# Loads of expert_w by rows, and two weight steps moved from the q/k/v part into the attention, in a pre-norm attention and MoE kernel

## The chip, the cores and the metric

The kernel runs on one core of a Trainium2 chip. The metric is the device time of one execution in microseconds (us). Before the change three runs gave a median of 2413.64 us (2413.22 to 2415.35).

The core has five engines with a queue of instructions each: TensorE (PE in the profile; PEld is its loading of weights), VectorE (DVE), ScalarE (ACT), GpSimd (POOL) and SyncE (SP). DMAs are issued here from SP and from POOL. The profile's q1 is the queue of the former, q0 that of the latter; both are worked on by the same 16 DMA engines.

## The reference

x has 2 x 2048 tokens of 1024 values in float32. The layer is an attention with one head of width 256 and a feed-forward part with a shared path and a routed path, which has one expert matrix and a gate:

```python
qkv = einsum('bsc,cf->bsf', layernorm(x), Wqkv) + bqkv          # 1024 x 768
attn = softmax(einsum('bqd,bkd->bqk', q, k) / sqrt(256))
x = x + einsum('bqd,dc->bqc', einsum('bqk,bkd->bqd', attn, v), Wo) + bo
h = layernorm(x)
shared = relu(h @ up_w) ** 2 @ down_w                             # 1024 x 2048 x 1024
routed = ((h @ fc1_w) @ expert_w * sum_top2(h @ gate_w)) @ fc2_w  # 1024 x 512 x 512 x 1024
x = x + layernorm2(shared + routed)                               # with ln_gamma, ln_beta
```

## The kernel before

Each float32 factor is split into two float32r parts, a high one (a cast on ACT) and a low one (a subtraction on DVE or POOL: `split`, L140). A product is then three matmuls (`Pass3`, L117). The 4096 tokens are 8 blocks of 512 rows. The work has four stages.

First, `begin` (L456) loads expert_w and both halves of fc2_w, and multiplies them once: expert_w @ fc2_w, the "fold" (`fold`, L487; tile pf). For that it needs expert_w with its rows along the free axis, so TensorE transposes it in 16 pieces of 128 x 128 (L478), four into one PSUM bank, and a bank is split into `eh` and `el`. expert_w lies in SBUF as `ew`, 128 partitions by 4 row groups of 512. Its four loads (L461) take 128 columns of all four row groups each. The queue of SP goes on with four loads of fc2_w's first half (L463), four rows of x, fc2_w's second half, and Wqkv. POOL loads the q/k bias and a broadcast of the v bias (bv). The second pass of the fold is interleaved with the transposes of the first block of x.

Second, `a_block` runs eight times in the order 4, 5, 6, 7, 0, 1, 2, 3 (`order`, L455). `qkv_block` (L406) computes four tiles of v (pv), then q and k (pq), and between these parts `after` normalises the next block: each of its four tiles is transposed by DVE in pieces of 32 x 32 (L213), written to DRAM by POOL (`xt_d`, L218), and fetched back by POOL in another order (`xt`, L224). The fourth tile's fetch is issued last, and its split comes after the next block's first tile of v. q is written to `q_d` by POOL (L448). In the last q/k/v block `after` also loads q_d of the first two blocks by SP (L663), and then come two loads of Wo (L701).

Third, the attention: for n from 1 to 8 the loop interleaves the scores of block n (`scores`, tile ps, two PSUM banks, a running maximum on DVE, L560) with the products of block n-1 with v (`values`, tile po), and ends with `finish` and `project` of block n-1 (tile pw, four PSUM banks). In `project` (L627) SP loads the residual x into `xres`, POOL adds bo to it by an accumulating DMA (L633), DVE adds the product (L644), and SP writes the sum to DRAM. POOL issues all four of these additions of a block ahead of what follows in its queue. A small load of gate_w (`g_f`, L704) precedes block 0's, and ACT and DVE split it (L749) in the middle of the first attention block.

Fourth, the feed-forward part multiplies quarters of the weights and of the activations in seven products where eight would be usual. It needs sums of quarters of up_w with fc1_w (s = 0) and of down_w with the fold (s = 1). These sums are made in DRAM by POOL's DMAs alone, in 14 steps (`sum_step`, L385):

```python
    SUMS = [(s, q) for s in range(2) for q in (1, 3, 2, 4)]
    COPIES = SUMS + [(s, q) for s in range(2) for q in ((0, 0), (1, 0), (1, 1))]
    ADDS = dict(zip((4, 5, 6, 8, 9, 10, 11, 13), SUMS))
```

A step copies one quarter (2 MB of up_w or down_w and 0.5 MB of fc1_w or of the fold, L389), and steps 4, 5, 6, 8, 9, 10, 11 and 13 then add another quarter, or a sum made before, to an earlier copy (L397, two DMAs again). Steps 0, 1 and 2 are taken after the blocks i = 4, 5 and 6 of the q/k/v part (L697). The others are taken in the attention, at k = 2 and k = 8 of each n from 2 on (L742), and are placed on POOL's queue directly behind the last bo addition of the block projected before (`last[0]`). So on POOL's queue they stand like this, with the bo additions of block b written as bo b:

```
q/k/v i=4: 0    i=5: 1    i=6: 2
g_f, bo 0 | 3 4+ | bo 1 | 5+ 6+ | bo 2 | 7 8+ | bo 3 | 9+ 10+ | bo 4 | 11+ 12 | bo 5 | 13+ | bo 6, bo 7
```

A plus marks a step with an addition. The numbers stand for copies; the additions go to `SUMS` in the order of `ADDS`.

Of the kernel before, what the change touches and what calls it, by code (L numbers as in the profile page):

```python
# [17 lines left out]
P = 128  # L18
# [7 lines left out]
def kernel(  # L26
# [21 lines left out]
    nc = tc.nc  # L48
# [3 lines left out]
    LAT = fc1_w.shape[1]  # L52
# [5 lines left out]
    NLC = LAT // P  # L58
    NKC = S // P
    NB = W // P  # L60
    NBLK = NT // W
# [105 lines left out]
    def cols(w, i, n):  # L167

        return w.rearrange("(c p) i -> p c i", p=P)[:, :, ts(i, n)]
# [213 lines left out]
    last = [None]  # L383
# [22 lines left out]
    def qkv_block(n, wqkv, xT, parts, after):  # L406

        keep = n < BPB  # L410
        units = {a: (unit if n == BPB - 1 else ex_unit)(f"{a}{n}") for a in "kv"}
        if keep:
            kv[n] = [units["k"], units["v"]]
        got = {}

        def v_tile(t):
            pm = bank(psa, "pv")
            if t % 2 == 0:
                got["v"] = half("v")
            acc = Pass3(pm[:, :D], NCC)  # L420
            for c in range(NCC):
                acc.add(x_chunk(xT, c, ts(t, P)), piece(wqkv[2], c, D, slice(0, D)))
            vt = got["v"][:, ts(t % 2, D)]
            nc.vector.tensor_tensor(vt, pm[:, :D], bv_sb, ALU.add)
            flush()
            split_late(vt, *(hl(units["v"])[:, s, ts(t, D)] for s in range(2)))

        def qk_chunk(a, dc):
            i = "qk".index(a)
            pm = bank(psa, "pq")  # L430
            acc = Pass3(pm, NCC)
            for c in range(NCC):
                acc.add(piece(wqkv[i], c, D, ts(dc, P)), x_chunk(xT, c))
            bias = bqk_sb[:, i * NDC + dc : i * NDC + dc + 1]
            flush()
            if a == "q":
                if dc == 0:
                    got["q"] = row("q")
                nc.scalar.activation(got["q"][:, ts(dc, W)], pm, AF.Identity, bias=bias)
            else:  # L440
                h, l = (hl(units[a])[:, s, ts(dc, W)] for s in range(2))
                nc.scalar.activation(h, pm, AF.Identity, bias=bias)
                nc.vector.scalar_tensor_tensor(l, pm, bias, f32(h), ALU.add, ALU.subtract)

        for j, (a, i) in enumerate(parts):
            v_tile(i) if a == "v" else qk_chunk(a, i)
            if (a, i) == ("q", NDC - 1):
                nc.gpsimd.dma_start(out=q_d[n], in_=got["q"])  # L448
            after(j)
        flush()  # L450
        if not keep:
            for a, d in (("k", k_d), ("v", v_d)):
                nc.gpsimd.dma_start(out=d[n], in_=f32(units[a]))

    order = list(range(BPB, NBLK)) + list(range(BPB))  # L455
    def begin(wqkv, xT):  # L456

        ew, f2_0 = (unit(a, FP) for a in ("ew", "f2_0"))
        ev = ew.rearrange("p (c n) -> p c n", n=LAT)
        for i in range(NLC):  # L460
            nc.sync.dma_start(out=ev[:, :, ts(i, P)], in_=cols(expert_w, i, P))  # L461
        for i in range(NLC):
            nc.sync.dma_start(out=f2_0[:, ts(i, W)], in_=fc2_w[ts(i, P), 0:W])  # L463
        f2 = [f2_0]
        first = load_block(xf, order[0])
        f2.append(load("f2_1", cols(fc2_w, 1, W))[1])

        ws = {i: load(f"w{i}", cols(Wqkv, i, D)) for i in (2, 0)}
        rows = load_block(xf, order[1])
        ws[1] = load("w1", cols(Wqkv, 1, D))  # L470
        nc.gpsimd.dma_start(out=bqk_sb, in_=bqkv[0 : 2 * D].rearrange("(f p) -> p f", p=P))
        nc.gpsimd.dma_start(out=bv_sb, in_=bqkv[2 * D : 3 * D].partition_broadcast(P))

        eh, el = unit("eh"), unit("el")
        for mc in range(NLC):
            pt = bank(psc, "pt")
            for lc in range(NLC):
                nc.tensor.transpose(pt[:, ts(lc, P)], ew[:, ds(lc * LAT + mc * P, P)], ident)  # L478
            split(pt, eh[:, ts(mc, LAT)], el[:, ts(mc, LAT)])

        def split_f2(h, eng):
            f2h, f2l = unit(f"f2h{h}"), unit(f"f2l{h}")
            for mc in range(NLC):
                split(f2[h][:, ts(mc, W)], f2h[:, ts(mc, W)], f2l[:, ts(mc, W)], eng)
            return f2h, f2l

        def fold(f2hl, first=None):  # L487
            accs = [Pass3(bank(psa, "pf"), NLC) for _ in range(NLC)]
            for mc in range(NLC):
                if first:  # L490
                    first(mc)
                for lc in range(NLC):
                    accs[lc].add(
                        piece((eh, el), mc, LAT, ts(lc, P)), piece(f2hl, mc, W, slice(0, W))
                    )
            return accs

        def folded(h, accs):
            r = unit(f"fold{h}", FP)
            for lc in range(NLC):  # L500
                nc.scalar.copy(r[:, ts(lc, W)], accs[lc].ps)
            return r

        accs = fold(split_f2(0, nc.vector))
        stats = [row_stats(first[0])]
        for t in range(NB):
            if t + 1 < NB:
                stats.append(row_stats(first[t + 1]))
            normalise(first[t], stats[t])
            if t == 0:  # L510
                f2hl = split_f2(1, nc.gpsimd)
            elif t == 2:
                wqkv[2] = split_unit(*ws[2], nc.gpsimd)
        r = [folded(0, accs)]
        r.append(folded(1, fold(f2hl, lambda t: transpose_tile(first[t], t, xT))))
        wqkv[0] = split_unit(*ws[0])
        wqkv[1] = split_unit(*ws[1], nc.gpsimd)
        return NormBlock(rows), r
# [167 lines left out]
    with tc.manual_schedule():  # L686
        norm, fold = begin(wqkv, xT)
        x3 = lambda: None
        steps = list(range(len(COPIES)))
        for i in range(NBLK - 1):  # L690
            norm, xT, x3 = a_block(i, norm, xT, x3)
            if i == 0:
                for h in range(C // W):
                    nc.gpsimd.dma_start(
                        out=cols(fc2e, h, W), in_=fold[h].rearrange("p (c n) -> p c n", n=W)
                    )
            if i >= NBLK // 2:  # L697
                sum_step(steps.pop(0))
    a_block(NBLK - 1, None, xT, x3)

# [6 lines left out]
    for n in range(1, NBLK + 1):  # L707
# [4 lines left out]
        for k in range(NKC + lag):  # L712
            if n + 1 < NBLK:
                if k == 0:
                    q_row = load_row(q_d[n + 1])
                elif k == NKC // 2:
                    start(n + 1, q_row)
            if n < NBLK and k < NKC:
                scores(n, k)
            if k >= lag:  # L720
                values(n - 1, k - lag)
                if n == BPB and (k - LAG) % 4 == 3:
                    j = BPB + (k - LAG) // 4
                    kv[j].append(load_kv(f"v{j}", v_d[j], kv_home(j)))
            if n == 1 and k == 1:
                softmax(0, 0)
            if n == 1 and k % 2 and 1 < k < NKC:
                softmax(0, k // 2)
            elif n > 1 and k % 2 == 0 and k + 2 < NKC:
                softmax(n - 1, k // 2 + 1)  # L730

            if k == NKC // 2 and n in range(2, 2 + NB):
                xts.append(load_row(x1[0][ts(n - 2, P), :]))
            elif k == 5 and n in range(3, 3 + NB):
                xts[n - 3] = norm_row(xts[n - 3], nc.sync)
            elif n == NBLK:
                if k < NB:
                    xts[k] = fetch_tile(xts[k], nc.sync)
                elif k % 2 == 0 and k >= 6 and k < 6 + 2 * NB:
                    for h, p in enumerate(X):  # L740
                        split_x(xts, h, k // 2 - 3, X[p])
            if k in (2, 8) and n > 1 and steps:  # L742
                with tc.issue_after(last[0].ins):
                    sum_step(steps.pop(0))
            if n == 1 and k == NKC // 2:
                wo = unit("wo_h"), unit("wo_l")
                for dc in range(NDC):
                    split(wo_f[dc], *(v[:, ts(dc, C)] for v in wo))
                split(g_f, gate[:, :, 0:NE], gate[:, :, NE : 2 * NE])  # L749
            if k == NKC - 1:  # L750
                if n == BPB - 1:
                    for j in range(BPB, 2 * BPB):
                        kv[j] = [load_kv(f"k{j}", k_d[j], kv_home(j))]
                if n < NBLK:
                    row_max(n)
# [532 lines left out]
```

## Time and profile before

| | us |
|---|---|
| median of three runs | 2413.64 |
| the profiled execution, its time | 2414.37 |
| its span, first to last instruction | 2412.4 |
| TensorE busy in the span | 2348.1 |

The stages in the span, with TensorE's and VectorE's busy time and the share of the 16 DMA engines:

| stage | from to | PE busy | DVE busy | DMA share |
|---|---|---|---|---|
| loads, fold | 0 to 40 | 31.25 | 20.83 | 0.76 |
| q/k/v | 40 to 320 | 271.83 | 155.13 | 0.73 |
| attention | 320 to 800 | 467.37 | 382.69 | 0.87 |
| feed-forward | 800 to 2412 | 1577.63 | 904.89 | 0.75 |

A matmul's end is modelled in the profile and matmuls overlap, so a busy TensorE is not one at its peak; its idle time is what shows a wait. The granted clock of TensorE (PEclk, 1.00 at full speed) falls for a while after some waits. A line of the timeline has the start and the duration in us, the engine, the line of the kernel, the operation, the tile written and those read, and in brackets how long the engine stood idle before and what ended that. For a DMA the duration is that of its issue; when its data has landed is told by the view of the DMAs.

### The profile page before, as it was taken

The numbers are of one execution on the slowest core, as the hardware profiler recorded it, in microseconds if no ns is written. First come the engines' busy times: TensorE is split into PE (matmuls) and PEld (weight loads), VectorE is DVE, ScalarE is ACT, GpSimd is POOL, SyncE is SP. The second block draws the span as 40 slices with busy tenths as digits, with TensorE's granted clock in tenths as the row PEclk, the third lists the DMA queues.
The fourth block names the chain that finished last, engine by engine and source line by source line (L and its number), as shares of the span: only waits on it lengthen the run. The fifth ranks groups of instructions, "written<-read, shape, count | busy, mean of one in ns | idle before, by whom it ended". The sixth has DMA issues, their size and how long they took to land.

```text
span 2412.4 us, 29279 instructions
## 1 busy us (share of the span) xinstructions
PE 2348.1 (97%) x10704; PEld 1922.9 (80%) x10704; DVE 1463.5 (61%) x2168; ACT 1131.3 (47%) x1846; POOL 299.5 (12%) x450
## 2 busy tenths in 40 slices
PE   8999899999998999999999999999999999999998
PEld 7888778888787778777777877777888887788886
DVE  5566549888777466687736458653446663445545
ACT  5555445555544553666552274544135354314224
POOL 3222110012110010011210011110000010000001
PEclk9999999999999999999999999999999999999999
DMA  5867883999996666677997778897557798655695
GB/s 186 320 245 266 286 201 110 287 317 320 285 244 183 214 230 184 230 244 243 337 307 237 239 265 316 316 333 259 194 184 266 257 325 292 212 194 185 203 310 189
DMA packets 225807, 603.99 MB, mean 250 GB/s; under 512 B 18768, under 2 KB 80720, under 8 KB 223616
## 3 DMA queue, kind: packets, MB, share of 16 engines
q1 hardware_dynamic: 152160, 334.02, 40.5%
q0 software_dynamic: 73504, 268.11, 36.3%
q8 instruction: 85, 1.39, 0.2%
q14 instruction: 58, 0.48, 0.1%
HBM read 448.96 MB, written 210.76 MB: 273 GB/s over the span
## 4 chain that ended last, share of the span: by engine, by line
PE 69%; issue 12%; DVE 6%; DMA 5%; ACT 5%; POOL 2%; POOLq 0%; SPq 0%; ACTq 0%; DVEq 0%
PE pu L130 28%; PE pd L130 21%; PE po L130 6%; PE ps L130 6%; PE pw L130 3%; DMA w<-wt 2%; DVE xblk L213 1%; DMA xres<-in_L_attn_bo_dram 1%; PE pg L870 1%; ACT xrow L283 1%; PE pf L130 1%; PE pq L130 1%; ACT junk L271 1%; DMA w_p<-w 1%; DVE w L821 1%
## 5 line engine op out<-in xcount | busy, mean ns | idle before, releaser
L130 PE MATMUL pd<-w,sp 128*128 128x512 f32 x3336 | 769.6, 392 | 18.8 <-DVE sp L1044 8.7
L130 PEld LDWEIGHTS pd<-w,sp 128*128 128x128 f32 x3336 | 625.8, 188 | 161.5 <-DVE sp L1044 18.0
L130 PE MATMUL pu<-xh,w 128*128 128x512 f32 x2240 | 692.9, 390 | 1.5 <-DVE w L821 0.8
L130 PEld LDWEIGHTS pu<-xh,w 128*128 128x128 f32 x2240 | 419.2, 188 | 92.4 <-DVE w L821 2.3
L130 PE MATMUL pu<-xl,w 128*128 128x512 f32 x1120 | 436.5, 390 | 2.9 <-DVE xl L150 2.8
L130 PEld LDWEIGHTS pu<-xl,w 128*128 128x128 f32 x1120 | 210.2, 188 | 48.3 <-DVE xl L150 4.6
L1044 DVE TENSOR_TENSOR sp<-h,sp 128x512 fp32r<-128x512 f32 x238 | 162.4, 687 | 128.2 <-ACT sp L1039 127.9
L1039 ACT CAST sp<-h 128x512 fp32r<-128x512 f32 x238 | 145.6, 618 | 182.7 <-PE pd L130 132.8
L130 PE MATMUL ps<-q,k 128*128 128x512 f32 x768 | 196.9, 394 | 3.7 <-DVE max L560 3.6
L130 PE MATMUL po<-p,v 128*128 128x512 f32 x768 | 197.2, 396 | 1.2 <-ACT p L142 1.1
L813 ACT CAST w<-w 128x512 fp32r<-128x512 f32 x210 | 128.1, 617 | 149.1 <-DMA w<-wt 140.3
L821 DVE TENSOR_TENSOR w<-w 128x512 fp32r<-128x512 f32 x210 | 142.8, 685 | 88.7 <-ACT w L813 87.0
L130 PEld LDWEIGHTS ps<-q,k 128*128 128x128 f32 x768 | 143.0, 189 | 38.5 <-DVE max L560 9.0
L130 PEld LDWEIGHTS po<-p,v 128*128 128x128 f32 x768 | 144.8, 190 | 31.9 <-ACT p L142 1.5
L824 POOL DMA_DIRECT2D w_p<-w x140 | 75.7, 541 | 586.6 <-DVE w L821 525.9
L992 ACT ACTIVATE h<-h 128x1024 f32<-128x1024 f32 x48 | 50.6, 1055 | 208.0 <-DVE h L1091 159.7
L555 ACT COPY s<-ps 128x512 f32<-128x512 f32 x128 | 75.0, 586 | 152.3 <-PE ps L130 148.9
L150 DVE TENSOR_TENSOR xl<-xt,xh 128x512 fp32r<-128x512 f32 x104 | 71.6, 688 | 120.8 <-ACT xh L149 120.7
L213 DVE STREAM_TRANSPOSE xblk<-xrow 128x1024 f32<-128x1024 f32 x60 | 120.4, 2007 | 39.1 <-ACT xrow L283 36.4
L560 DVE TENSOR_TENSOR max<-ps,max 128x512 f32<-128x512 f32 x120 | 82.4, 687 | 45.2 <-ACT s L555 45.1
L130 PE MATMUL pq<-xha,w_h 128*128 128x512 f32 x256 | 99.7, 389 | 0.0
L130 PE MATMUL pq<-xha,w_l 128*128 128x512 f32 x256 | 99.7, 389 | 0.0
(181 smaller groups left out, 3040.7 us busy)
## 6 DMA issues: line engine op xcount, KB each, us to landing
w<-w_p SPq DMA_DIRECT2D x350, 512.0 KB, 4.3
w_p<-w POOLq DMA_DIRECT2D x140, 512.0 KB, 4.7
w<-wt SPq DMA_DIRECT2D x210, 256.0 KB, 3.6
xt_d<-xblk POOLq DMA_DIRECT2D x56, 512.0 KB, 3.5
xt<-xt_d POOLq DMA_DIRECT2D x56, 512.0 KB, 6.3
wt<-in_L_ffn_up_w_dram POOLq DMA_DIRECT2D x9, 2048.0 KB, 24.9
wt<-in_L_ffn_down_w_dram POOLq DMA_DIRECT2D x9, 2048.0 KB, 34.1
xres<-in_L_attn_x_dram SPq DMA_DIRECT2D x32, 512.0 KB, 12.4
```

The costliest lines, as they stand in the source:

```text
L130: nc.tensor.matmul(self.ps, lhsT=a, rhs=b, start=self.i == 0, stop=self.i == self.n - 1, skip_group_check=self.on,)
L150: late_ops.append(lambda: nc.vector.tensor_tensor(lo, t, f32(hi), ALU.subtract))
L213: nc.vector.transpose(b.rearrange("p (q k i) -> p q k i", q=P // SQ, i=SQ), r.rearrange("p (k i q) -> p q k i", k=NCC, i=SQ),)
L271: nc.scalar.activation(self.junk(), self.v, AF.Square, bias=self.nm, accum_out=s2)
L555: nc.scalar.copy(s["s"][k // 4][:, ts(k % 4, W)], pm)
L560: nc.vector.tensor_tensor(s["max"], pm, s["max"], ALU.max)
L813: nc.scalar.copy(w[:, 0:W], f32(w)[:, W : 2 * W])
L821: nc.vector.tensor_tensor(w[:, W : 2 * W], v[:, W : 2 * W], v[:, 0:W], ALU.subtract)
L824: nc.gpsimd.dma_start(out=kept[key], in_=w.bitcast(FP))
L992: nc.scalar.activation(o, v, AF.Relu)
L1039: nc.scalar.copy(t[:, 0:W], v)
L1044: add(t[:, W : 2 * W], v, f32(t)[:, 0:W], ALU.subtract)
```

## The change

expert_w's four loads take 128 whole rows each, 2 KB to a row, where they took 128 columns of all rows, 512 bytes at a time. The transposes go through row groups on the outside: a bank gets the four pieces of one row group, and its split is written in pieces of 128 columns to all four parts of `eh` and `el`. The fold's first twelve matmuls, one round over its four accumulators, therefore read pieces from all four banks, where they read the first bank's alone.

In the q/k/v part only i = 4 takes a step. In the attention n = 1 takes one, at k = 8; `last[0]` is the write of `q_d` then, since no bo addition has been issued. From n = 2 on two are taken as before, through n = 7.

```diff
             if (a, i) == ("q", NDC - 1):
-                nc.gpsimd.dma_start(out=q_d[n], in_=got["q"])
+                last[0] = nc.gpsimd.dma_start(out=q_d[n], in_=got["q"])
             after(j)
...
         ew, f2_0 = (unit(a, FP) for a in ("ew", "f2_0"))
-        ev = ew.rearrange("p (c n) -> p c n", n=LAT)
         for i in range(NLC):
-            nc.sync.dma_start(out=ev[:, :, ts(i, P)], in_=cols(expert_w, i, P))
+            nc.sync.dma_start(out=ew[:, ts(i, LAT)], in_=expert_w[ts(i, P), :])
...
         eh, el = unit("eh"), unit("el")
-        for mc in range(NLC):
+        for lc in range(NLC):
             pt = bank(psc, "pt")
-            for lc in range(NLC):
-                nc.tensor.transpose(pt[:, ts(lc, P)], ew[:, ds(lc * LAT + mc * P, P)], ident)
-            split(pt, eh[:, ts(mc, LAT)], el[:, ts(mc, LAT)])
+            for mc in range(NLC):
+                nc.tensor.transpose(pt[:, ts(mc, P)], ew[:, ds(lc * LAT + mc * P, P)], ident)
+            hi, lo = (v.rearrange("p (m l) -> p m l", l=LAT)[:, :, ts(lc, P)] for v in (eh, el))
+            split(pt.rearrange("p (m l) -> p m l", l=P), hi, lo)
...
-            if i >= NBLK // 2:
+            if i == NBLK // 2:
                 sum_step(steps.pop(0))
...
-            if k in (2, 8) and n > 1 and steps:
+            if k in (2, 8)[-n:] and steps:
                 with tc.issue_after(last[0].ins):
                     sum_step(steps.pop(0))
```

The matmuls, the casts and the subtractions keep their number and their order. POOL's queue has the steps at these places:

```
q/k/v i=4: 0
q_d of block 3, 1, g_f, bo 0 | 2 3 | bo 1 | 4+ 5+ | bo 2 | 6+ 7 | bo 3 | 8+ 9+ | bo 4 | 10+ 11+ | bo 5 | 12 13+ | bo 6, bo 7
```

## Prediction

> **What bounds the kernel now.** I read the page first, then the waits of TensorE over the whole span, then each wait's stretch in the timeline, and last the landings of the transfers. The page says that TensorE is nearly always at work, so a change can win only what is left of its idle time, some 64 us, or lose by making more of it.
>
> ```profile
> PE 2348.1 (97%) x10704; PEld 1922.9 (80%) x10704; DVE 1463.5 (61%) x2168; ACT 1131.3 (47%) x1846; POOL 299.5 (12%) x450
> ```
>
> TensorE's waits (first column after the arrow the releaser, then us in total, times, longest) name four places before the feed-forward part:
>
> ```profile
> PE pt L478 <- DMA ew<-in_L_ffn_expert_w_dram: 7.6, 2, 3.8
> PE psum L617 <- DVE sum L593: 7.4, 1, 7.4
> PE pv L130 <- ACT xha L142: 6.1, 1, 6.1
> PE ps L130 <- DVE max L560: 3.6, 3, 1.8
> ```
>
> The first is at the start. In the timeline the transposes of expert_w run in two pairs, and the second pair waits for the third load; the first product of the fold comes at 12.63:
>
> ```profile
> 3.78 1.94 PE L478 MATMUL pt<-ident,ew 128*128 128x128 f32 x8 [3.78 <-DMA ew<-in_L_ffn_expert_w_dram]
> 9.50 1.94 PE L478 MATMUL pt<-ident,ew 128*128 128x128 f32 x8 [3.78 <-DMA ew<-in_L_ffn_expert_w_dram]
> 12.63 0.80 PE L130 MATMUL pf<-f2h,eh 128*128 128x512 f32 x1 [1.19 <-ACT f2h L142]
> ```
>
> The third (6.1 us, at 282.5 to 288.6, in the last q/k/v block) waits for the fourth tile of x. Of the POOL queue there:
>
> ```profile
> 279.38 0.77 POOL L224 DMA_DIRECT2D xt<-xt_d  x1 [6.30 <-issue]
> 280.14 0.56 POOL L448 DMA_DIRECT2D q_d<-q  x1
> 280.69 0.66 POOL L389 DMA_DIRECT2D wt<-in_L_ffn_up_w_dram  x1
> ```
>
> The fetch landed at 286.3. It was issued only when the write of its tile (271.79) had landed, at 278.9; that write met the two loads of q_d (SP, 271.52). The third weight step stands behind the fetch.
>
> The fourth has its dearest case in the attention, where bo's rows are added to the residual by POOL's DMAs (L633) and VectorE uses them (L644). For block 4 VectorE waits, for block 5 not:
>
> ```profile
> 629.71 0.75 DVE L644 SCALAR_TENSOR_TENSOR xres<-pw,ri,xres 128x512 f32<-128x512 f32 x1 [3.40 <-DMA xres<-in_L_attn_bo_dram]
> ...
> 687.12 0.75 DVE L644 SCALAR_TENSOR_TENSOR xres<-pw,ri,xres 128x512 f32<-128x512 f32 x1 [1.00 <-PE pw L130]
> ```
>
> In the windows behind block 4's wait (PE busy is the second number, PEclk the last but two) TensorE loses 1.80 us of four, and then the clock (0.68 in the next window):
>
> ```profile
> 638.00:640.00 2.00, 0.96 (x5) 0.46 (x3) 2.00 (x3) 0.59 (x1) 0.00 (x0) 1.00 1.07 317
> 640.00:642.00 2.00, 1.24 (x5) 1.07 (x6) 2.00 (x4) 0.00 (x0) 0.00 (x0) 0.97 1.05 311
> 642.00:644.00 2.00, 2.00 (x6) 1.51 (x6) 2.00 (x2) 0.59 (x1) 0.00 (x0) 0.50 1.03 297
> ```
>
> By single issues in the DMA view, block 4's four bo rows landed at 629.5, 632.0, 634.5 and 637.5, some 31 us after their issue, and block 5's at 677.3, 679.6, 682.2 and 684.7. Block 5's were 9.8 to 10.5 us ahead of VectorE (687.1, 690.0, 692.5, 695.2 by the same spacing). The DMA share is 1.01 to 1.13 in every 5-us window from 560 to 705, and 0.00 to 0.76 from 715 to 750.
>
> **What the Trainium skill says.** "DMA: Bandwidth & Descriptors", section Queues, rings and completion order: an engine takes one queue's descriptors in ring order and goes round its queues packet by packet. The trace agrees: block 4's bo rows land 2.5 to 3.0 us apart directly behind the last sum (627.1). The same page, Specifications, has 512 B as the least size for full rate. Here the trace's packet records say less: at the start a 512-B packet takes 27 ns and a 2048-B one 84, so 2 KB in pieces cost 108. "TensorE: Matmul & The Clock Gate", Part 1, lets the clock fall to half after an idle window of about 3.4 us. The trace has 0.50 after the 6.1-us wait and even after 1.8 us in two gaps.
>
> **Part 1, expert_w by rows.** The same four loads of 256 KB, in 512 packets of 2048 B and not 2048 of 512 B. Engine time: 2048 x 27 ns / 16 = 3.5 us before, 512 x 84 / 16 = 2.7 after. From 4.5 us the 128-KB broadcast of bv puts 32 packets of 4096 B with about 0.9 us each among them (1.8 us per engine); before, 60 to 70% of expert_w had gone by then, after, about 85% will have. Two of SP's loads of x waited for loads of expert_w (2.0 us in the waits of SP), so these come earlier as well. I put the fourth load at 6 to 7.5 us. TensorE's 16 transposes, the ACT casts (586 ns) and VectorE subtractions (692 ns) keep number and size; two PSUM banks and those two engines let the third transpose start at 6.2 and the fourth end near 8.3. Then the first cast of fc2_w, which needs its load (landed 10.8 before; two queue effects give 9 to 9.5), so the fold starts at about 9.9, not 12.63: 2.7 us. A few matmuls fewer at the cold 427 ns: 0.3. Together -3.0; bounds -0.8 (fc2_w's load hardly moves) and -4.5. Rows of x, fc2_1 and the V weights have 5 to 9 us in hand, so nothing else is late first. Strided writes of eh and el in pieces of 512 B: no row shows them; nothing, at most +0.3.
>
> **Part 2, the moves.** Step 1 leaves 244.64, step 2 leaves 280.69. Step 1's copies landed at 261.9, before the transfers that matter (263.3 on); step 2's stand behind the fetch in one ring, and the last fetches of the two blocks before (207.25 and 241.22), with a step behind them too, took 4.6 us each. So the 6.1-us wait stays: 0, at best -8.5 (6.1 and 2.4 of slow clock in 286 to 294).
>
> In the new order on POOL, step 1 (two DMAs as ever, 2 MB of up_w and 0.5 MB of fc1_w, 1.3 us of issue) stands between the write of q_d for the last block (309.23) and the load of g_f, then come block 0's bo rows, and steps 2 and 3. A copy alone is 2.5 MB, about 8.2 us (328.3 to 336.5 by packets), with a load of x between 9.6; g_f would land at about 323.7 and not 314.2, and ACT's cast of it stands at 323.77 ahead of a copy of scores. Taken +0.3; bounds 0 and +2. The bo rows behind it are needed at 395.
>
> From there every slot holds other steps. With a sum at 640 packets x 327 ns / 16 = 13.1 us (from a sum; 4 KB) or 1280 x 176 / 16 = 14.1 (from down_w and fc2e; 2 KB), and copies near 6.4 to 8.2:
> - before block 2's and block 3's bo rows: the same units, within 1 us.
> - before block 4's: two copies and sums of 14.1 and 14.1 before, of 13.1 and 14.1 after: 1 us less. VectorE's 3.4 us become 2.4; TensorE's 2.0 idle become about 0.9, and the 1.7 us of slow clock go: -2.8.
> - before block 5's: copy, sum 13.1, copy before; copy, sum 14.1, copy, sum 13.1 after. With the 1 us from above the rows land 13.1 later: 690.4, 692.7, 695.3, 697.8. The first needs to be there at 687.1 - 2.8 = 684.3. VectorE waits 6.1 us; the four PSUM banks took up 1.4 of 3.4 at block 4, so TensorE loses 4.7, and 2.4 by the clock as in the last q/k/v block: +7.1. Bounds 0 (the margin holds) and +10.
> - before block 6's: one copy more. Rows at about 740 to 748 instead of 716.4 to 726.5, needed from 742.8 + 4: hidden, narrowly, by the idle DMA of 715 to 745. If that cover is gone, VectorE waits as at block 5.
> The sums are wanted in the feed-forward part after 769, when the queue is empty again; its 7.4-us wait there is for a fresh weight load and stays.
>
> **Sum.** -3.0 + 0 + 0.3 - 2.8 + 7.1 = +1.6 us, on the profiled execution's 2414.37 (span 2412.4, with 2.0 around it) 2416.0; that execution stood 0.7 above the median 2413.64, so 2415.2. A difference within 0.2% (4.8 us) can't be told from none for this kernel.
>
> **Rivals.**
> - The last q/k/v block's wait goes with the copies. For: the step is issued within it, and shares the memory. Against: ring order, and that SP's loads explain it. 2415.2 - 8.5 = 2406.7. Chance 0.08.
> - The margin holds at block 5. For: the DMA idles at 715 to 745, so there is room in all. Against: it is behind the place where the rows are due. 2415.2 - 7.1 = 2408.1. Chance 0.10.
> - The slow side: the ring's backlog outlasts block 6 too. One mechanism: bo's rows in order behind 26 us of copies and a sum. Price: another wait like block 4's, 3.7, and about 2 more at block 5: 2420.9. It decides from where block 5's rows land 2 us later than I put them (sums at 14 and not 13.1 us, twice, are enough). For: only 6 us of margin at block 6. Against: the queue's work from 547 to 627 summed to 73 of 80 us with such prices. Chance 0.30.
> - The forecast, no measurable change: 0.52. That the move doesn't happen is excluded by the changed order of the queue.
>
> **How the numbers follow.** The likeliest is 2415.2, its own range 2411 to 2418.4. The range 2408 to 2422 leaves out the first rival and the far end of the third, under 0.2. Faster: the first two rivals, 0.17 (the second lies just over the bound). Slower: 0.30 and a little of the forecast's upper edge, 0.31. Same: 0.52.
>
> **What would show it.** Part 1: first fold product near 9.9, the waits for ew gone. Part 2: the 6.1-us wait still there, g_f landing near 323; VectorE's wait for bo at block 4 shorter, a new one of 5 to 7 us near 684 to 690 with the clock at half behind it; DMA busy to about 745. I am wrong if the last q/k/v block no longer waits, if block 5's rows land before 685 (less 3), or if block 6 waits.

## The result, and the profile after

The changed kernel takes 2423.81 us, the median of 4 runs (2420.89 to 2428.3), beside 2413.43 of the kernel before: a ratio of 1.0043, with a 95% interval of 1.003 to 1.0056. That is slower, by about 10 us, where the prediction had 2415.2 and a range up to 2422. The profiled execution is the run of 2428.3 us, the longest of the four; its span is 2426.2. Measured once more (r_after below), the change costs a little less: 2421.08 beside 2412.27, ratio 1.0035 (1.0022 to 1.0047).

The page of the kernel after first. Busy time hardly moves (TensorE 2351.1 us, where it had 2348.1), so most of what was lost is idle time:

```profile
PE 2351.1 (97%) x10704; PEld 1925.2 (79%) x10704; DVE 1463.5 (60%) x2168; ACT 1130.8 (47%) x1846; POOL 298.2 (12%) x450
```

TensorE's waits of the kernel after (releaser behind the arrow, then us in total, times, longest):

```profile
PE psum L617 <- DVE sum L593: 8.4, 1, 8.4
PE pv L130 <- ACT xha L142: 7.6, 1, 7.6
PE pt L477 <- DMA ew<-in_L_ffn_expert_w_dram: 6.6, 2, 3.6
...
PE pw L130 <- DVE xres L644: 4.3, 1, 4.3
```

The wait for expert_w is still 6.6 us of 7.6. The wait in the last q/k/v block has not gone with the sum step, it has grown from 6.1 to 7.6. New is the last line: a projection that waits for VectorE's residual addition (L644). In the timeline of VectorE at block 5 one sees what that addition waited for:

```profile
689.89 1.41 DVE L644 SCALAR_TENSOR_TENSOR xres<-pw,ri,xres 128x512 f32<-128x512 f32 x2 [8.27 <-DMA xres<-in_L_attn_bo_dram]
```

Two gaps of TensorE follow from it, one in the projection itself, and one at a score, which waits for the running maximum that stands behind the late additions in VectorE's queue:

```profile
690.70 0.74 PE L130 MATMUL pw<-wo_h,o 128*128 128x512 f32 x2 [4.26 <-DVE xres L644]
704.36 1.65 PE L130 MATMUL ps<-q,k 128*128 128x512 f32 x6 [1.45 <-DVE max L560]
```

Single issues in the DMA view give block 5's bo rows as landed at 689.8, 692.3, 694.8 and 698.8 (predicted 690.4, 692.7, 695.3, 697.8; before 677.3 to 684.7). The windows of 2 us there (PE busy second; the last three numbers are PEclk, DMA share and GB/s) show TensorE running dry and then paying with its clock:

```profile
686.00:688.00 2.00, 0.43 (x2) 0.01 (x1) 0.00 (x0) 0.00 (x0) 0.38 (x1) 1.00 1.05 207
688.00:690.00 2.00, 0.00 (x0) 0.00 (x0) 0.11 (x1) 0.00 (x0) 0.18 (x1) 1.00 1.09 217
690.00:692.00 2.00, 1.30 (x5) 1.06 (x6) 2.00 (x3) 0.00 (x0) 1.04 (x1) 0.88 1.03 250
692.00:694.00 2.00, 2.00 (x6) 1.58 (x5) 2.00 (x3) 0.00 (x0) 0.84 (x1) 0.50 1.04 338
694.00:696.00 2.00, 2.00 (x8) 1.59 (x7) 2.00 (x4) 0.00 (x0) 0.65 (x1) 0.77 1.00 397
```

A busy PE of 2.00 with 6 matmuls, at a PEclk of 0.50, is the half clock; the three windows from 680 to 686, at 1.00, have 10 or 11. The DMA engines are full (1.0 and above) all the while. Block 6 does not wait: its rows land at 737.4 to 744.8, its projection starts at 744.95, and the DMA engines are all but idle by then (0.08):

```profile
730.00:735.00 5.00, 5.00 (x24) 4.14 (x23) 2.17 (x4) 1.46 (x3) 0.00 (x0) 1.00 1.05 208
735.00:740.00 5.00, 5.00 (x26) 3.82 (x25) 1.89 (x3) 0.59 (x1) 0.00 (x0) 1.00 0.56 111
740.00:745.00 5.00, 5.00 (x34) 4.46 (x32) 4.08 (x4) 3.28 (x5) 0.00 (x0) 1.00 0.08 15
```

Both kernels issue the same 10704 matmuls in the same order, so a run can be laid beside another matmul by matmul. The table has the start of some of them, in us from the span's start, in all profiles of the two kernels and in those of four experiments. `pw4` is the first projection matmul of block 4, and so on; the last column is the feed-forward part, from its first matmul to the end of the last.

| profile | fold | first v | pw0 | pw4 to pw5 | pw5 to pw6 | pw6 to ff | feed-forward |
|---|---|---|---|---|---|---|---|
| before | 12.63 | 40.28 | 393.42 | 60.06 | 57.46 | 59.14 | 1600.15 |
| before, again | 12.30 | 40.24 | 393.32 | 55.85 | 57.45 | 60.26 | 1601.44 |
| after | 11.71 | 39.03 | 393.17 | 55.86 | 65.40 | 60.57 | 1608.81 |
| after, again | 11.37 | 38.47 | 392.41 | 59.25 | 65.90 | 60.16 | 1599.22 |
| e1_rows | 10.86 | 38.03 | 391.20 | 55.86 | 57.47 | 61.40 | 1599.64 |
| e2_moves | 12.23 | 39.59 | 393.08 | 55.86 | 64.44 | 59.62 | 1601.70 |
| e3_layout | 10.71 | 38.49 | 391.95 | 56.37 | 65.67 | 61.30 | 1602.91 |
| e4_slots | 10.90 | 38.01 | 391.81 | 55.96 | 57.45 | 59.33 | 1600.54 |

From pw0 to pw4 all eight take 230.5 to 230.6 us. Column by column the table tells the rest. Block 5 (pw5 to pw6) costs 7.0 to 8.4 us more in every run with the moved steps as the change moves them, and in no other. Block 4 (pw4 to pw5) has its wait in one profile of the kernel before and not in the other, and the same holds of the kernel after. The five profiles with the rows of expert_w reach block 0 (pw0) 0.15 to 2.1 us ahead of the second profile of before, 1.2 on the mean. And the feed-forward part, 8.7 us longer in the first profile of after, is not longer in the second.

### The profile page after: what moved, and what is told of

The parts are those of the page before. It is cut to its first block, busy times and chain, and to the rows that moved or that the text cites. A ratio compares the mean times of both kernels' runs of the same rounds, so it can differ in the third digit from the quotient of the medians.

```text
span 2426.2 us, 29276 instructions
## 1 busy us (share of the span) xinstructions
PE 2351.1 (97%) x10704; PEld 1925.2 (79%) x10704; DVE 1463.5 (60%) x2168; ACT 1130.8 (47%) x1846; POOL 298.2 (12%) x450
## 4 chain that ended last, share of the span: by engine, by line
PE 69%; issue 9%; DMA 8%; DVE 7%; ACT 6%; POOL 1%; SPq 0%; POOLq 0%; ACTq 0%; DVEq 0%
PE pu L130 28%; PE pd L130 21%; PE po L130 6%; PE ps L130 6%; PE pw L130 3%; DMA w<-wt 2%; DVE xblk L213 2%; DMA xres<-in_L_attn_bo_dram 2%; ACT xrow L283 1%; DMA xt_d<-xblk 1%; PE pg L870 1%; ACT junk L271 1%; PE pf L130 1%; DVE sp L1044 1%; DVE w L821 1%
## 5 line engine op out<-in xcount | busy, mean ns | idle before, releaser
L130 PE MATMUL pu<-xh,w 128*128 128x512 f32 x2240 | 694.8, 391 | 3.8 <-DVE w L821 2.1
```

What stands on the lines that cost most here:

```text
L130: nc.tensor.matmul(self.ps, lhsT=a, rhs=b, start=self.i == 0, stop=self.i == self.n - 1, skip_group_check=self.on,)
```

## The experiments

Open after the first profile were three things: whether the loss comes from the moved steps alone, why so little came of expert_w's rows and of the removal of a step from the last q/k/v block, and what made the feed-forward part longer. For the last a suspect was at hand: if DRAM tiles get their addresses in the order of their first use in the program, which no run here shows, the moved steps shift many of them.

**e1_rows** is the kernel before with the hunks of `begin` alone.

> Before with the rows of expert_w alone; both sum steps stay in the q/k/v stage. In the trace of after the fold starts at 11.7 us instead of 12.6 and the first v tile at 39.0 instead of 40.3. Theory A (the whole loss of after comes from the moved steps): the end comes 0.9 to 1.6 us earlier than before, 2411.8 to 2412.5 us; blocks 4 and 5 of the attention and the feed-forward stage as in before. Theory B (the rows themselves bring part of the loss, by shifting the later stages against the DMA traffic): 2414 us or more, with the first pv still at 39.0.

Measured: 2411.11 us beside 2412.75 (ratio 0.9995, 0.9987 to 1.0003), blocks and feed-forward as in before. Theory A. The rows are worth some 1.2 us by the ratio and 1.6 by the medians, though the interval does not exclude that they are worth nothing.

**e2_moves** is the kernel before with the other three hunks alone.

> Before with the moved sum steps alone; expert_w by columns as before. Theory A: first fold at 12.6 us, block 4's wait for bo gone (-3 to -4), block 5 waits for bo for about 4 + 1.5 us with the clock gap behind it (+8), feed-forward entered about 6 us later than before; total 2419 to 2424 us, that is after plus 1 us. Theory B: less than 2417 us.

Measured: 2419.14 us (ratio 1.0029, 1.0017 to 1.004). The moves lose 6.4 us by themselves (by the medians; 7.0 by the ratio): theory A. But this run was expected to be a microsecond worse than the whole change, and it is not: the rows, added to the moves, gain nothing. In the table e3_layout, with the rows of expert_w, enters block 5 0.6 us earlier than e2_moves and leaves it 0.6 us later: where the landing of bo sets the end of the block, a start won upstream is waited away.

**e3_layout** gives every DRAM tile of after the place in the order of first use that it has in before:

```diff
             if i == NBLK // 2:
                 sum_step(steps.pop(0))
+            elif i > NBLK // 2:
+                place(i - 4)
...
                     sum_step(steps.pop(0))
+                    if k == 8 and n > 1 and steps:
+                        place(steps[0])
```

where `place(i)` copies 16x64 numbers into each tile of step i.

> After, with all DRAM tiles at the addresses of before (two tiny copies ahead of each moved step take the tile's place early). If the placement in DRAM is what costs time in the feed-forward stage: that stage takes 1611 to 1613 us as in before, and the total is before + 5, 2418 to 2419 us, with little spread. If the feed-forward stage pays for the way it is entered (later, with DMA work pushed back): the stage takes 1613 to 1621 us again, total 2420 to 2428 us with the wide spread of after.

Measured: 2422.16 us (ratio 1.0039, 1.0026 to 1.0051), as slow as after. So the placement is not the cause, as far as the order of first use decides it. The feed-forward part took 1614.4 us to the end of the span (1602.91 by the table's measure), at the near end of what the other theory gave; whether that theory holds was left to the next two runs.

**r_after** and **r_before**, the two kernels unchanged, each with a new profile, on the same chip.

> After once more, unchanged, beside a profile of before on the same chip. If the extra time in the feed-forward stage (1620.7 us in the first profile of after, 1611.7 in before) belongs to the change, its profile has about 1620 us there again; if most of it was chance, it has 1612 to 1615 us, as in the two runs of e2_moves and e3_layout (1613.6, 1614.4). Total 2419 to 2426 us. Block 5 waits for its last bo row for 7 to 8 us with the clock gap behind it, in either case.

> Before once more, unchanged. Feed-forward stage 1611 to 1612 us. If block 4's wait for bo (2.8 us) belongs to the kernel, it is there again; if it stands on an edge, as the runs e1_rows and e4_slots without it suggest, the rows of bo land at or before 627 us and it is gone, and the total is about 2410 us instead of 2413.

Measured: after 2421.08, before 2411.97 us. After's feed-forward part is 1599.22 us, the shortest of the table, and 1611.1 to the end of the span, although it is entered later than in any other profile of the table (at 808.25). A late entry alone does not lengthen it, and what the first profile showed there belonged to that execution. Block 4's wait has changed sides. In the second profile of before the rows of bo land at 625.0, 627.4, 629.9 and 632.5, and VectorE does not wait for them:

```profile
626.75 0.75 DVE L644 SCALAR_TENSOR_TENSOR xres<-pw,ri,xres 128x512 f32<-128x512 f32 x1 [0.63 <-PE pw L130]
```

In the second profile of after they land at 628.9 to 637.2, and it does:

```profile
629.12 0.75 DVE L644 SCALAR_TENSOR_TENSOR xres<-pw,ri,xres 128x512 f32<-128x512 f32 x1 [3.87 <-DMA xres<-in_L_attn_bo_dram]
```

With the first profiles (before 629.5 to 637.5, after 625.7 to 633.4) each kernel was seen on both sides of the edge. The clock is no surer. TensorE has one gap behind this wait, first in the first profile of before, then in the second of after, whose window follows:

```profile
640.76 2.01 PE L130 MATMUL ps<-q,k 128*128 128x512 f32 x6 [1.80 <-DVE max L560]
```

```profile
640.51 1.65 PE L130 MATMUL ps<-q,k 128*128 128x512 f32 x6 [2.13 <-DVE max L560]
642.00:644.00 2.00, 2.00 (x10) 1.69 (x9) 2.00 (x2) 0.59 (x1) 0.00 (x0) 1.00 1.08 291
```

The gap of 1.80 us was followed by half clock (the prediction shows the window, 0.50), the longer one of 2.13 by none. The total of before did not follow as expected: 2411.97, and not 2410.

**e4_slots** lets n = 2 take three steps, so that from n = 3 on every block has the steps it had before the change, and steps 1 and 2 still stay out of the q/k/v part.

```diff
-            if k in (2, 8)[-n:] and steps:
-                with tc.issue_after(last[0].ins):
-                    sum_step(steps.pop(0))
+            for _ in range((1 + (k == 2 and n == 2)) * (k in (2, 8)[-n:])):
+                if steps:
+                    with tc.issue_after(last[0].ins):
+                        sum_step(steps.pop(0))
```

> After, but block n=2 of the attention takes three steps (2, 3 and 4 with its sum), so that from block 3 on each block has the steps it had in before; steps 1 and 2 stay out of the q/k/v stage. If the wait in block 5 comes from the sums being one slot later: bo of block 5 lands at 677 to 685 us, no wait there, block 4's wait of about 3 us is back; feed-forward entered within 1.5 us of before and total 2411.5 to 2414 us. If leaving the q/k/v stage costs by itself (g_f, Wo, scores), the first pw of block 1 comes later than 393.4 and the total is above 2416 us. If steps 1 to 4 together outlast block 2, g_f or bo of blocks 1 to 2 wait, seen as an idle gap before pw at 452 to 510 us.

Measured: 2411.24 us (ratio 0.9992, 0.9984 to 1.0). Block 5's rows land at 673.1 to 680.6 and VectorE waits only for TensorE there:

```profile
681.36 0.75 DVE L644 SCALAR_TENSOR_TENSOR xres<-pw,ri,xres 128x512 f32<-128x512 f32 x1 [1.00 <-PE pw L130]
```

The whole loss of the change is undone by pulling one step forward, to the time of e1_rows (2411.11), which also has the rows. Two steps leaving the q/k/v part cost nothing that the totals show; that every later step came one place later does. Of block 4's wait, expected back, hardly anything is there: the rows land at 625.4, right on the edge, and VectorE stands idle 0.91 us ahead of them, where 0.63 is usual.

**e5_spread** goes further, three copies in n = 1 and only one step in n = 3.

```diff
-            if k in (2, 8)[-n:] and steps:
-                with tc.issue_after(last[0].ins):
-                    sum_step(steps.pop(0))
+            for _ in range({(1, 2): 0, (1, 8): 3, (3, 8): 0}.get((n, k), k in (2, 8))):
+                if steps:
+                    with tc.issue_after(last[0].ins):
+                        sum_step(steps.pop(0))
```

> After, with the steps spread over the idle DMA of blocks 1 and 2: block n=1 takes the copies 1 to 3, n=2 the sums of 4 and 5, n=3 that of 6 alone, n=4 steps 7 and 8; from n=5 on as in before. If the waits of blocks 4 and 5 come from the sums queued ahead of bo: rows of block 4 land by about 610 us and of block 5 by about 680 us, neither waits, feed-forward entered 4 to 6 us before that of before, total 2408.5 to 2411 us. If g_f, now behind three copies, is waited for (DVE or ACT idle before the split at about 350 us, then scores), pw of block 0 comes after 394 us and the total is above 2413 us.

Measured: 2431.72 us (ratio 1.0082, 1.0068 to 1.0095), the second case and the worst run of all. No wait at blocks 4 and 5, but one of 17.7 us on ScalarE, and one of 16.8 us on TensorE behind it (the last line, from TensorE's waits: the releaser, then us in total, times, longest):

```profile
339.68 0.24 ACT L142 CAST gate<-g_f 128x64 fp32r<-128x64 f32 x1 [17.70 <-DMA g_f<-in_L_ffn_gate_w_dram]
...
PE ps L130 <- DVE max L560: 18.6, 3, 16.8
```

Although the steps stand at k = 8 in the text, POOL issues them as soon as the write of q_d lets it, and g_f's load comes behind all three:

```profile
307.88 0.64 POOL L389 DMA_DIRECT2D wt<-in_L_ffn_up_w_dram  x1
...
310.96 0.63 POOL L389 DMA_DIRECT2D wt<-in_L_ffn_fc_w_dram  x1
311.60 0.92 POOL L704 DMA_DIRECT2D g_f<-in_L_ffn_gate_w_dram  x1
```

g_f is 32 KB. Behind 7.5 MB of copies in one ring it landed 28.1 us after its issue, at 339.7; behind one step, in after, 14.3. The Trainium skill, "DMA: Bandwidth & Descriptors", section Queues, rings and completion order, has an engine take one queue's descriptors in ring order; it says so of the queues of SP and ACT, and this run agrees for POOL's with its 28.1 us. Behind ScalarE's cast stood the copies of scores, for which TensorE waited.

**e6_late** is e4_slots with SP's loads of q_d 0 and 1 and of Wo handed to POOL's queue, behind the last fetch of x:

```diff
+                elif j == NB - 1:
+                    nxt.extend(load_row(q_d[m], nc.gpsimd) for m in range(2))
                 elif j == 2 * NB - 1:
-                    start(0, load_row(q_d[0]))
+                    start(0, nxt[0])
...
-                    start(1, load_row(q_d[1]))
+                    start(1, nxt.pop())
+                    nxt.clear()
...
-    wo_f = [load_row(Wo[ts(dc, P), :]) for dc in range(NDC)]
+    wo_f = [load_row(Wo[ts(dc, P), :], nc.gpsimd) for dc in range(NDC)]
```

> The kernel of e4_slots with SP's loads of q_d 0 and 1 and of Wo moved to POOL's queue behind the last fetch of xt. If SP's loads are what slows the last xt_d write (8.6 us from issue to landing) and fetch (6.9 us): these take about 5 us each, the 7.6 us wait of the last v tile falls to 0 to 4 us and the total is 4 to 8 us below that of e4_slots, 2404 to 2407.5 us. If the write and the fetch are slow by POOL's own queue, the wait stays at 6 to 8 us and the total is 2410 to 2413 us. If the loads are now too late for the scores, the first score comes later than 318 us.

Measured: 2403.66 us (ratio 0.997, 0.9958 to 0.9981), 7.6 us below e4_slots (measured on another chip, where before was 0.5 us slower). POOL's and SP's queues in after, and then POOL's in e6_late, at the same place. The write (L218) is the fourth tile's; the first fetch (L224) is the third tile's, the second the fourth's:

```profile
270.11 0.53 POOL L218 DMA_DIRECT2D xt_d<-xblk  x1 [2.96 <-DVE v L150]
270.63 0.77 POOL L224 DMA_DIRECT2D xt<-xt_d  x1
279.22 0.77 POOL L224 DMA_DIRECT2D xt<-xt_d  x1 [7.82 <-DMA xt_d<-xblk]
...
269.85 0.83 SPq L192 DMA_DIRECT2D xrow<-q_d  x2
278.69 0.83 SPq L192 DMA_DIRECT2D xrow<-in_L_attn_Wo_dram  x2
```

```profile
269.12 0.53 POOL L218 DMA_DIRECT2D xt_d<-xblk  x1 [2.94 <-DVE xblk L213]
269.65 0.77 POOL L224 DMA_DIRECT2D xt<-xt_d  x1
272.56 0.77 POOL L224 DMA_DIRECT2D xt<-xt_d  x1 [2.15 <-DMA xt_d<-xblk]
```

In after the write took 8.6 us from issue to landing and the fetch 6.9; in e4_slots 7.0 and 8.0; with SP's four loads out of the way 2.9 and 5.1. The write takes 6.9 to 8.6 us in all nine profiles with SP's loads there, and 2.9 in all four without, e6_late and the three kernels below. The 7.1-us wait of e4_slots for the fourth tile (7.6 in after) is gone, and so is the slow clock behind it. The scores start at 308.49, not later but 8 us earlier than in e4_slots (316.89).

Three more kernels build on e6_late. **e8_spread_gf** takes the steps of e5_spread, but puts those of n = 1 behind g_f: `last[0]` becomes g_f's load.

> The kernel of e6_late with the steps spread as in e5_spread, but the steps of block n=1 put behind g_f's load on POOL. If ACT's 17.7 us wait for g_f was the whole of e5_spread's loss: no wait at 326 us, the bo rows of block 4 land 10 us or more before they are needed, and the total is that of e6_late less 0 to 3 us (block 4's edge), 2400.5 to 2404 us. If three copies at 320 us cost something else as well (q rows, bo of block 0), pw of block 0 or 1 comes late and the total is above 2406 us.

Measured: 2402.52 us (ratio 0.9961, 0.9949 to 0.9974). g_f lands at 304.0, its cast waits for nothing, and e5_spread's loss is gone: g_f was all of it. Block 4's rows land at 611.9, 4.8 us ahead of VectorE (616.67), half of what was expected. They stand behind the steps of n = 5, which e8_spread_gf leaves alone, and the DMA engines are full (a share of 1.01 or more in every 5-us window) from 530 to 615. In e9_bv, which keeps the steps of e6_late, they land at 613.6, so that what the spread wins there is no more than the scatter.

**e9_bv** moves one line of `begin`:

```diff
-        nc.gpsimd.dma_start(out=bv_sb, in_=bqkv[2 * D : 3 * D].partition_broadcast(P))
...
                 f2hl = split_f2(1, nc.gpsimd)
+                nc.gpsimd.dma_start(out=bv_sb, in_=bqkv[2 * D : 3 * D].partition_broadcast(P))
```

> The kernel of e6_late with the 128-partition broadcast of bv issued after the first split of fc2_w on POOL, at about 19 us, instead of at 2.6 us. If bv's slow packets hold the last pieces of expert_w back: the transposes no longer wait at 5 to 8.6 us for more than 1 us, the first fold starts at 8.5 to 9.5 us instead of 10.6 to 11.7, and the total is 1 to 2 us lower than that of e6_late. If the DMA rate of the loads themselves sets it, the fold starts at 10.5 us or later and the total is unchanged. If bv now lands after 38 us, the first v tile waits for it and the gain is lost.

Measured: 2402.72 us (ratio 0.996, 0.9948 to 0.9973), not to be told from e6_late. The fold starts at 10.10 instead of 10.64, and the transposes still wait:

```profile
PE pt L476 <- DMA ew<-in_L_ffn_expert_w_dram: 4.8, 3, 3.5
```

That lies between the two cases of the expectation. Moving bv goes with a fold 0.5 us earlier here, and 0.7 us in e10_all beside e8_spread_gf (10.35 and 11.03), less than the kernels with bv in its place differ among themselves (10.64 to 11.71). The totals show nothing of it.

> e8_spread_gf and e9_bv together. If their effects are independent the total is that of e6_late plus the two differences, 2399 to 2403 us.

**e10_all** measured 2402.19 us (ratio 0.9959, 0.9945 to 0.9973). The four kernels from e6_late on can't be told apart; all beat both kernels of this study, before by 9 to 11 us.

## Why the prediction was wrong

The prediction's sum was -3.0 + 0 + 0.3 - 2.8 + 7.1. Its losses were right, its gains were not there. The steps that failed are two terms, "Together -3.0" of Part 1 and the "-2.8" before block 4, and the adding of the first of them to a wait that takes it back.

- **Part 1** was mis-sized: the fourth load was put at 6 to 7.5 us and the fold at 9.9; in the two profiles of after the fourth load landed at 8.96 both times, and the fold starts at 11.71 and 11.37. At the first v tile the five profiles with rows stand 1.2 to 2.2 us ahead of the second profile of before, at pw0 0.15 to 2.1 (1.2 on the mean), and e1_rows gains 1.2 to 1.6 in the total. The kernel after loses a part of it again at the last q/k/v block: the fourth tile's write was issued 1.7 us earlier than before (270.11 against 271.79) and landed only 0.2 earlier (278.7 against 278.9). That does not come of the earlier start, since in e1_rows, as early (269.5), the write took 7.0 us; why it took 8.6 and 8.3 in after is open. Open too is why the last of expert_w's pieces come so late; bv's broadcast, which the prediction charged, is not the main reason.
- **The sum itself.** The prediction took block 4's 2.8 us off the time at which block 5's rows are due (687.1 - 2.8) and left their landing at 690.4, but it did not take off Part 1's 3.0. By its own figures a start 3.0 us earlier makes that wait 3.0 us longer, so that the sum should have been +4.6 and not +1.6. e2_moves and e3_layout agree with that: what the rows won is gone when block 5 ends.
- **The last q/k/v block's wait** stays, as forecast: it is there in after and in e4_slots (7.6 and 7.1 us), with no step behind the fetch, which refutes the rival that had it go. And the reason given, SP's loads, is the right one, as e6_late shows.
- **g_f** landed at 324.6 (forecast 323.7), and the +0.3 was right: TensorE has a gap of 0.58 and of 0.74 us near 326 in the two profiles of after, and none there in before. e5_spread shows that it is an edge too, with 17 us behind it.
- **Block 4, -2.8.** The term read one execution's wait as the kernel's. The rows land within about 6 us of each other from one execution to the next. The 1 us less of sums in the queue can't be seen beside that, and the wait is there or not in both kernels. The 1.7 us of slow clock in the term are no surer: the prediction saw two gaps ahead of it, but it was a single one of 1.80 us, and after one of 2.13 in the second profile of after the clock stayed at 1.00. None of it can be counted as a gain of the change.
- **Block 5, +7.1.** Right in mechanism and size: 7.9 us lost on the mean of four profiles (57.45 against 65.40, 65.90, 64.44 and 65.67), of which in the first profile of after 5.7 are TensorE's two gaps (forecast 4.7) and 1.7 the clock (forecast 2.4). The rows were predicted to within 1 us in that profile; in the second they landed 2.8 to 4.2 us later. e4_slots removes the loss by the queue alone.
- **Block 6** hidden: right. The slow rival, whose 2420.9 lies near the measured times, named the wrong mechanism, and the nearness is chance: even in the second profile of after, with block 5's rows as late as that rival asked, no backlog outlasts block 6, nor does it in any other run.
- **Feed-forward, 0.** Not contradicted. The first profile alone would have said +8.7. The four profiles with the steps moved as the change moves them have 1603.2 us on the mean and the other four of the table 1600.4, a difference well within what two profiles of after differ by (9.6).

With the measured sizes the sum is -1.2 + 7.9 = +6.7. The medians differ by 8.8 and 10.4, e2_moves and e3_layout by 6.4 and 9.4. The 2 to 3.7 us between are not traced to a place: 27 runs of before go from 2408.39 to 2415.51 us, 4 runs of after from 2420.89 to 2428.3 and 5 more from 2417.52 to 2421.39, and both block 4's edge and the feed-forward part (1599 to 1609 us) vary by as much.

## What to carry to other kernels

When steps on a DMA ring are postponed, look for the due time of every small transfer that will stand behind them (bo's rows, g_f), not at the total load: the DMA engines were idle at 740 us, and the time was lost at 690. Before a wait is counted as something to be won, look at its margin: one that ends within the scatter of the landings is there in one execution and gone in the next, so it belongs in the range and not in the sum; and a start that is won ahead of a wait for DMA is worth only as much as that DMA comes earlier too. When a transfer on the critical path is slow, look at what the other queues issue at that moment: loads without a near due time can go behind it.

## What was not expected of the hardware

A 512-KB write that takes 2.9 us from issue to landing took 6.9 to 8.6 us when another queue had issued two loads of the same size just before it, though the second queue held only 1 MB. The landing of the same rows, in the same program, moved by 4.5 us between two executions (629.5 and 625.0, with TensorE 0.2 us apart and the DMA engines full since 560). A gap of TensorE of 1.80 us was followed by half clock, and one of 2.13 us at the same place in another execution was not. And moving a broadcast with slow packets off the start of the kernel gained at most 0.7 us there, where its packets' time (1.8 us per DMA engine) had seemed to be in the way.
